# The second layer's normalisation tail, one round shorter: squares a round earlier, and inverse roots as one GpSimd power

## The chip, the cores and the metric

The kernel runs on one core of a Trainium2 chip. The core has five engines that run side by side, each through its own queue in order: TensorE (in the profile PE, with its weight loads as PEld), VectorE (DVE), ScalarE (ACT), GpSimd (POOL) and SyncE (SP), which here only issues DMAs. An instruction waits at the head of its queue until what it reads has been written and what it overwrites has been read; everything behind it waits too. The metric is the device time of one execution in microseconds, lower is better, given as the median over several runs.

## What is computed

Two transformer layers on an input `x` of 8 sequences with 256 rows of 512. Each is an attention and a feed-forward part, with residuals. The change lies in the attention of the second layer, an mLSTM with 16 heads of 32 columns; `q` is the normalised input, `k` and `v` are a given context:

```python
D = jnp.exp(log_D - max_log_D)
qk = jnp.einsum('bhsd,bhtd->bhst', qh, kh) / jnp.sqrt(dh)
C = qk * D
normalizer = jnp.maximum(jnp.abs(C.sum(-1, keepdims=True)), jnp.exp(-max_log_D))
Cn = C / (normalizer + EPS)
h = jnp.einsum('bhst,bhtd->bhsd', Cn, vh)
mu = h.mean(-1, keepdims=True)
var = ((h - mu) ** 2).mean(-1, keepdims=True)
hn = (h - mu) * jax.lax.rsqrt(var + EPS)
hn = hn * ln_scale.reshape(1, nh, 1, dh)
```

`x` plus this result is normalised again (a layer norm, then the RMS norm of the mixture of 32 experts that follows), routed to four experts a row, and added up.

## The kernel before, in words

The stages follow one another: first layer's attention (0 to about 235 us), its feed-forward part (to about 405 us), second layer's attention (to about 600 us), routing and the experts (to the end). Each stage begins while the former drains.

In the second layer's attention a **batch** is one sequence (256 rows, two tiles of 128 rows, j = 0 and 1, held in `g.X[2b]` and `g.X[2b+1]`), and a **block** is a batch and four of its heads. There are 32 blocks, and `round_` (L916) is called with a rising n. The order in which it issues work is kept as written on TensorE, ScalarE, VectorE and GpSimd (`manual_schedule`, L1040). A round n does, for different blocks at a time:

- `decays`: TensorE products and ScalarE exponentials for block n (`xe`, L732);
- `back` (L779): for block n - 3, the heads' results turned back to rows, and copied by ScalarE into `hid[b]` (L787);
- `weights` (L740): for block n - 1, TensorE's `pqk` (L747, L751), then on VectorE two products `ct` (L755);
- `heads` (L761): for block n - 2, TensorE's `num`, read from `ct`;
- `tail` (L867): the normalisation of the batches whose four blocks are done.

`hid[b]` is complete in round n = 6 + 4b. The tail of batch b counts r from there, so r = n - 6 - 4b, and in each round up to four batches are at different r, the older first (r of 8 and up, then 4 to 7, then 0 to 3; r of 12 and up at the round's end). Before the change:

- r = 0, `scales` (L794): ScalarE takes the absolute values of the normaliser's column, VectorE the maximum `nm` (L799).
- r = 1, `squares` (L802): GpSimd squares `hid` into `sq` (L805; for the last batch ScalarE, L807), ScalarE squares `nm` (L808).
- r = 2, `variance` (L811): VectorE sums `sq` by head (L812) and adds `nm` (L813).
- r = 3 and 4, `rsqrt` (L82): an inverse square root on VectorE from an integer guess and three Newton steps, 11 instructions of 128x36 (L89 to L94). 32 of the 36 columns are this batch's heads; the other four belong to the norms of the batch before it.
- r = 4: `shifts` (L830) makes those norms' offsets `nb` on VectorE (L832), with one small addition on GpSimd (L837). Then `attended` (L817): GpSimd multiplies `hid` by the roots (L819, 1,024 columns), and for each of the two tiles by `ln_scale` (L824) and adds it to `x` (L825).
- r = 6 and 7: VectorE's statistics of the two tiles (`norm_stats`, L101 and L102), and in r = 7 the two variances (L900, L901) into the four columns of the next batch's `var`. The last batch has no next one and takes its own `rsqrt` and `shifts` there (L902).
- r = 11 and 12, `normed` (L840): ScalarE writes the normalised tile `yn` (L843), GpSimd scales `x` (L844), SP stores `yn` to `h_d` (L847).
- r = 13 and 14, `turned` (L850): TensorE transposes the tile (`hT`, L854), ScalarE copies it (L856).

The blocks end with round 34; 15 rounds more drain the tail (L1042, `full` is 35). Into some of the drain's rounds `filler` (L1027) puts products of the shared expert on TensorE (`pgu` L961, `po` L981) with their VectorE parts (`act` L970, `x` L989). After the loop come the logits (L1003), the remaining fillers, routing and the experts.

GpSimd has two further pieces of work in this stage: in rounds 24 and 26 a product over 1,024 columns for the shared expert's weights (`scale_shared`, L1240). And from round 3 on each round takes one step of the second half of the gates (`Gates.chain`, L495; its steps on VectorE include L508 to L523, and the splits into three parts, L528 and L530).

Of the kernel before, what the change touches and what calls it, by code (L numbers as in the profile page):

```python
# [19 lines left out]
F32 = mybir.dt.float32  # L20
# [4 lines left out]
AF = mybir.ActivationFunctionType  # L25
ALU = mybir.AluOpType
# [4 lines left out]
P = 128  # L31
D = 512
KD = D // P
B = 8
# [47 lines left out]
def rsqrt(g, x, n):  # L82


    nc = g.nc
    r = g.small.tile([P, n], F32, tag="rsq", name="rsq")
    t = g.small.tile([P, n], F32, tag="rsqt", name="rsqt")
    ri = r.bitcast(I32)
    nc.vector.tensor_scalar(ri, x.bitcast(I32), 1, None, ALU.arith_shift_right)  # L89
    nc.vector.tensor_scalar(ri, ri, -1, 0x5F3759DF, ALU.mult, ALU.add)  # L90
    for n in range(3):
        nc.vector.tensor_mul(t, r, r)
        nc.vector.scalar_tensor_tensor(t, t, -0.5, x, ALU.mult, ALU.mult)
        nc.vector.scalar_tensor_tensor(r, t, 1.5, r, ALU.add, ALU.mult)  # L94
        yield r


def norm_stats(g, mv, x):

    st = g.small.tile([P, 6], F32, tag="st", name="st")  # L100
    g.nc.vector.bn_stats(st, x)  # L101
    g.nc.vector.bn_aggr(mv, st)  # L102
# [10 lines left out]
def setup(g, ctx, tc):  # L113
    nc = g.nc
    g.const = const = ctx.enter_context(tc.tile_pool(name="const", bufs=1, reuse_waits="tile"))
    g.small = ctx.enter_context(tc.tile_pool(name="small", bufs=4, reuse_waits="tile"))
    xp = ctx.enter_context(tc.tile_pool(name="resid", bufs=1, reuse_waits="tile"))
    g.X = [xp.tile([P, D], F32, tag=f"x{i}", name=f"x{i}") for i in range(NT)]

    g.ident = const.tile([P, P], F32, tag="ident", name="ident")  # L120
    make_identity(nc, g.ident)
    g.identb = const.tile([P, P], BF16, tag="identb", name="identb")
    nc.vector.tensor_copy(g.identb, g.ident)
    g.ones = const.tile([P, S], F32, tag="ones", name="ones")
    nc.vector.memset(g.ones, 1.0)
    g.eps = {}
    for n, v in (("ln", 1e-5), ("gn", 1e-3), ("n", 1e-6 * math.sqrt(1e-6)), ("magic", MAGIC), ("-magic", -MAGIC)):
        t = const.tile([P, 1], F32, tag=f"eps_{n}", name=f"eps_{n}")
        nc.vector.memset(t, v)
        g.eps[n] = t  # L130
# [545 lines left out]
def layer1_attention(g, tc, gates):  # L676
    nc = g.nc
    with ExitStack() as ctx:
# [19 lines left out]
        with tc.tile_pool(name="a1ps2", bufs=1, space=PSUM, reuse_waits="tile") as ps, tc.tile_pool(name="a1work", bufs=2, reuse_waits="tile") as work:  # L698
# [90 lines left out]
            shape = [P, 2 * H1, HD1]  # L789

            def flat(hid):
                return hid.rearrange("p j h d -> p (j h) d")[:, :, :HD1]

            def scales(b, hid):  # L794


                nm = g.small.tile([P, 2, H1], F32, tag="nm", name="nm")
                nc.scalar.activation(nm, hid[:, :, :, HD1], AF.Abs)
                nc.vector.tensor_max(nm, nm, em[:, :, b * H1 : (b + 1) * H1])  # L799
                return nm  # L800

            def squares(b, hid, nm):  # L802
                sq = work.tile(shape, F32, tag="sq", name="sq", bufs=1)
                if b + 1 < B:
                    nc.gpsimd.tensor_mul(sq, flat(hid), flat(hid))  # L805
                else:
                    nc.scalar.activation(sq, flat(hid), AF.Square)  # L807
                nc.scalar.activation(nm, nm, AF.Square, bias=g.eps["n"], scale=math.sqrt(1e-6))  # L808
                return sq

            def variance(var, sq, nm):  # L811
                nc.vector.tensor_reduce(var, sq, AX.X, ALU.add)  # L812
                nc.vector.scalar_tensor_tensor(  # L813
                    var, var, 1.0 / HD1, nm.rearrange("p j h -> p (j h)"), ALU.mult, ALU.add
                )

            def attended(b, hid, rs):  # L817

                nc.gpsimd.tensor_mul(flat(hid), flat(hid), rs.unsqueeze(2).to_broadcast(shape))  # L819
                for j in range(2):  # L820
                    i = 2 * b + j
                    hj = hid[:, j, :, :HD1]
                    x, scale = (t.rearrange("p (h d) -> p h d", d=HD1) for t in (g.X[i], lns))
                    nc.gpsimd.tensor_mul(hj, hj, scale)  # L824
                    nc.gpsimd.tensor_add(x, x, hj)  # L825
# [4 lines left out]
            def shifts(mv, rs):  # L830
                nb = g.small.tile([P, 2, 2], F32, tag="nb2", name="nb2")
                nc.vector.scalar_tensor_tensor(  # L832
                    nb, mv[:, :, 0].unsqueeze(1).to_broadcast([P, 2, 2]), -1.0,
                    rs.rearrange("p (n j) -> p n j", n=2), ALU.mult, ALU.mult,
                )

                nc.gpsimd.tensor_scalar(rs[:, :2], rs[:, :2], 1.0, None, ALU.add)  # L837
                return nb
# [11 lines left out]
            def turned(i, h):  # L850

                pt = ps.tile([P, CH], F32, tag="dec", name="hT", bufs=2).rearrange("p (k t) -> p k t", k=KD)
                for k in range(KD):
                    nc.tensor.transpose(pt[:, k, :], h[:, k * P : (k + 1) * P], g.ident)  # L854
                c, o = divmod(i * P, CH)
                nc.scalar.copy(qT[c][:, :, o : o + P], pt)  # L856
# [5 lines left out]
            V, hid, xe, ct, num, numT = {0: values(0)}, {}, {}, {}, {}, {}  # L862
            nm, sq, v, mv, nb, h, roots = {}, {}, {}, {}, {}, {}, {}
            end = KD - 1 + 3
            NV = 2 * H1

            def tail(n, r0, of):  # L867

                for r in (r0 + 4 * m for m in of):
                    b, rest = divmod(n - end - r, KD)  # L870
                    if rest or not 0 <= b < B:
                        continue
                    if r == 0:
                        nm[b] = scales(b, hid[b])
                    if r == 1:
                        sq[b] = squares(b, hid[b], nm[b])
                    if r == 2:
                        v[b] = g.small.tile([P, NV + 4], F32, tag="var", name="var")
                        variance(v[b][:, :NV], sq.pop(b), nm.pop(b))
                        if b == 0:  # L880
                            nc.vector.memset(v[b][:, NV:], 1.0)
                    if r == 3:
                        roots[b] = rsqrt(g, v[b], NV + 4)
                        next(roots[b])
                    if r == 4:
                        next(roots[b])
                        rs = v[b] = next(roots[b])
                        if b:
                            nb[b - 1] = shifts(mv[b - 1], rs[:, NV:])
                        attended(b, hid.pop(b), rs[:, :NV])  # L890
                    if r in (6, 7):
                        if r == 6:
                            mv[b] = g.small.tile([P, 2, 2], F32, tag="mv2", name="mv2")
                        norm_stats(g, mv[b][:, r - 6], g.X[2 * b + r - 6])
                        if r == 7:
                            if b + 1 == B:
                                v[B] = g.small.tile([P, NV + 4], F32, tag="var", name="var")
                                nc.vector.memset(v[B], 1.0)
                            rt = v[b + 1][:, NV:].rearrange("p (n j) -> p n j", n=2)
                            nc.vector.tensor_scalar(rt[:, 0], mv[b][:, :, 1], 1e-5, None, ALU.add)  # L900
                            nc.vector.tensor_scalar(rt[:, 1], mv[b][:, :, 1], 1.0 + 1e-6, 1e-11, ALU.mult, ALU.add)  # L901
                            if b + 1 == B:  # L902
                                *_, v[B] = rsqrt(g, v[B], NV + 4)
                                nb[b] = shifts(mv[b], v[B][:, NV:])
                    if r in (11, 12):
                        i = 2 * b + r - 11
                        h[i] = normed(i, v[b + 1][:, NV:].rearrange("p (n j) -> p n j", n=2), nb[b])
                    if r in (13, 14):
                        turned(2 * b + r - 13, h.pop(2 * b + r - 13))

            second = gates.chain(
                1, lambda: ps.tile([P, 2, CH], F32, tag="pqk", name="gates", bufs=2)[:, :, :S],
# [107 lines left out]
            for c in range(EARLY):  # L1020
                of = [(p, r) for p, r in chunk(c)]
# [17 lines left out]
            E_ = mybir.EngineType  # L1039
            with tc.manual_schedule(engines={E_.PE, E_.Activation, E_.DVE, E_.Pool}):  # L1040
                full = len(blocks) + 3
                for n in range(full + 15):  # L1042
                    round_(n)
                    if n >= full and n - full in (0, 1, 2, 4, 5, 8, 9):
                        filler()
                logits_turned(logits())
# [495 lines left out]
```

## Time and profile before

| | |
|---|---|
| median of 3 runs | 1127.02 us (1123.28, 1127.02, 1127.94) |
| the profiled execution's own time | 1118.39 us |
| its span, first to last instruction | 1116.6 us |
| granted TensorE clock over the span | 0.964 |
| TensorE busy | 1019.6 us (91%) |
| VectorE busy | 524.3 us (47%) |
| ScalarE busy | 396.4 us (36%) |
| GpSimd busy | 390.6 us (35%) |

The profile describes one execution. Its span leaves out 1.8 us that lie around the first and last instruction. It also gives, in slices or windows of time, how long each engine was busy and which share of the full TensorE clock was granted. The view of waits lists which instruction waited for which, with the sum, the number and the longest. The chain of waits follows the work that ended last back from the end of the program. In lines that describe groups, "x64" is the number of instructions, followed by busy time and mean duration, and by the idle time before them and what ended it. By stage, in windows (us):

| window | length | TensorE busy | VectorE busy | GpSimd busy | granted clock |
|---|---|---|---|---|---|
| 420.00 to 484.60 | 64.60 | 53.69 | 42.77 | 13.49 | 0.87 |
| 484.60 to 560.20 | 75.60 | 66.15 | 50.83 | 44.09 | 0.91 |
| 560.20 to 619.00 | 58.80 | 54.53 | 24.65 | 29.57 | 0.97 |
| 619.00 to 668.00 | 49.00 | 44.68 | 47.25 | 5.74 | 0.97 |
| 668.00 to 1116.60 | 448.60 | 430.19 | 90.97 | 216.52 | 0.98 |

The first two are the blocks of the second layer's attention, the third is the drain of its tail, the fourth the routing, the last the experts.

### The profile page before, as it was taken

What the parts mean: (1) busy time and instruction counts of PE and PEld (TensorE: products, weight loads), DVE (VectorE), ACT (ScalarE), POOL (GpSimd) and SP (SyncE); (2) the same over time, 40 slices, a digit from 0 to 9 for tenths busy, and PEclk for the clock granted to TensorE, in tenths of its full rate; (3) what the DMA queues carried; (4) which work ended last, traced back from release to release, by engine and by line L of the source; (5) the groups of instructions that cost most, each with busy time, mean ns of one, the idle gap of its engine ahead of it and who ended that gap; (6) DMA issues with size and microseconds to landing.
All of it is one profiled execution on the core that took longest, in us unless ns stands there. A gap on an engine that the chain in (4) does not pass through costs nothing.

```text
span 1116.6 us, 14778 instructions
## 1 busy us (share of the span) xinstructions
PE 1019.6 (91%) x5219; PEld 617.4 (55%) x5234; DVE 524.3 (47%) x1480; ACT 396.4 (36%) x680; POOL 390.6 (35%) x367
## 2 busy tenths in 40 slices
PE   7989799988999768798889899999999999999994
PEld 5756466643444344455544444555566666677782
DVE  6545545468988744876653893121211212121210
ACT  4455335145666455457542100221122222312111
POOL 0144522230000100346464203644555555545432
PEclk9999899999999988889899999999999999999997
DMA  9686411013222211212012234877777788899982
GB/s 348 252 282 223 140 65 48 1 29 71 54 53 54 46 48 42 66 61 69 30 47 104 62 138 137 196 183 194 199 203 198 193 212 215 237 233 241 233 217 35
DMA packets 101107, 152.31 MB, mean 136 GB/s; under 512 B 39684, under 2 KB 42372, under 8 KB 101000
## 3 DMA queue, kind: packets, MB, share of 16 engines
q1 hardware_dynamic: 81872, 106.68, 30.9%
q0 software_dynamic: 18912, 44.50, 18.2%
q8 instruction: 43, 0.70, 0.3%
q14 instruction: 40, 0.33, 0.1%
q10 hardware_dynamic: 240, 0.10, 0.0%
HBM read 110.42 MB, written 32.96 MB: 128 GB/s over the span
## 4 chain that ended last, share of the span: by engine, by line
PE 67%; DVE 11%; DMA 7%; POOL 5%; ACT 5%; issue 3%; SPq 0%; DVEq 0%; POOLq 0%; ACTq 0%
PE po L1291 13%; PE pg L1274 12%; PE pu L1274 12%; PE p L557 3%; PE pz L372 3%; PE pw L317 3%; PE pt L1331 3%; DMA hqT<-hq 2%; DVE ct L755 2%; DMA raw<-in_ctx 2%; PE pqk L747 1%; PE pd L727 1%; PE num L768 1%; PE po L981 1%; PE py L576 1%
## 5 line engine op out<-in xcount | busy, mean ns | idle before, releaser
L1279 DVE TENSOR_TENSOR act<-pu,sg 128x264 f32<-128x264 f32 (+22 forms) x68 | 31.9, 469 | 314.9 <-PE pu L1274 308.7
L1316 POOL DMA_INDIRECT xg<-h_d,tok_of x85 | 83.6, 983 | 198.5 <-DVE of L1326 63.8
L1335 POOL DMA_INDIRECT out_x<-eo,to x85 | 132.9, 1564 | 55.4 <-ACT eo L1373 34.9
L1291 PE MATMUL po<-w,act 128*128 128x512 f32 (+10 forms) x456 | 143.1, 490 | 0.0
L1274 PE MATMUL pg<-xT,w 128*128 128x216 f32 (+21 forms) x512 | 136.5, 410 | 0.8 <-issue 0.8
L1274 PE MATMUL pu<-xT,w 128*128 128x216 f32 (+21 forms) x512 | 133.3, 403 | 0.0
L1373 ACT ACTIVATE eo<-po,slotw 128x512 f32<-128x512 f32 (+10 forms) x114 | 65.7, 577 | 178.1 <-PE po L1291 171.7
L1274 PEld LDWEIGHTS pg<-xT,w 128*128 128x128 f32 x512 | 93.9, 191 | 34.2 <-issue 18.8
L1274 PEld LDWEIGHTS pu<-xT,w 128*128 128x128 f32 x512 | 96.8, 190 | 26.2 <-issue 5.6
L1278 ACT ACTIVATE sg<-pg 128x264 f32<-128x264 f32 (+22 forms) x68 | 28.5, 419 | 203.7 <-PE pg L1274 188.2
L1291 PEld LDWEIGHTS po<-w,act 128*128 128x128 f32 (+10 forms) x456 | 54.1, 155 | 57.4 <-issue 47.9
L557 PE MATMUL p<-wq,xqT 128*128 128x512 bf16 (+1 forms) x379 | 79.5, 361 | 3.2 <-DMA xqT<-xq 2.1
L755 DVE SCALAR_TENSOR_TENSOR ct<-pqk,xe 128x768 f32<-128x768 f32 x64 | 58.3, 952 | 38.1 <-PE pqk L751 19.5
L557 PEld LDWEIGHTS <-xqT 128*128 128x128 bf16 x384 | 36.7, 98 | 44.4 <-DMA xqT<-xq 6.4
L1332 DVE TENSOR_TENSOR xT<-pt,nw 128x512 f32<-128x512 f32 (+12 forms) x85 | 51.1, 601 | 21.5 <-PE pt L1331 21.5
L317 PE MATMUL pw<-wg,xnT 128*128 128x512 f32 x128 | 60.9, 621 | 0.0
L732 ACT ACTIVATE xe<-pd 128x512 f32<-128x512 f32 x96 | 54.6, 596 | 13.6 <-PE pd L728 12.7
L372 PE MATMUL pz<-wo,wyT 128*128 128x512 f32 x128 | 57.9, 595 | 1.6 <-ACT wyT L366 1.6
L1331 PEld LDWEIGHTS pt<-ident,xg 128*128 128x128 f32 (+15 forms) x340 | 39.2, 140 | 25.2 <-PE po L1291 10.5
L101 DVE BATCH_NORM_STATS2 st<-x 128x6 f32<-128x512 f32 x64 | 43.8, 685 | 16.1 <-POOL x L825 10.1
L1331 PE MATMUL pt<-ident,xg 128*128 128x128 f32 (+15 forms) x340 | 47.2, 260 | 1.7 <-DVE xT L1332 1.7
L576 PE MATMUL py<-wq,hqT 128*128 128x512 bf16 x168 | 41.2, 380 | 7.8 <-DMA hqT<-hq 7.4
(289 smaller groups left out, 1636.6 us busy)
## 6 DMA issues: line engine op xcount, KB each, us to landing
w<-in_w SPq DMA_DIRECT2D x32, 1024.0 KB
w<-in_w SPq DMA_DIRECT2D x32, 512.0 KB
wst<-in_w1T SPq DMA_DIRECT2D x8, 704.0 KB
wst<-in_w3T SPq DMA_DIRECT2D x8, 704.0 KB
wst<-in_w2T SPq DMA_DIRECT2D x6, 768.0 KB
x<-in_x SPq DMA_DIRECT2D x16, 256.0 KB
ctxT<-in_ctxT_d SPq DMA_DIRECT2D x4, 1024.0 KB
raw<-in_ctx SPq DMA_DIRECT2D x16, 256.0 KB
```

The source lines that it names most:

```text
L317: nc.tensor.matmul(pw, lhsT=xnT[c][:, k, o : o + P], rhs=wg[:, k, :], start=k == 0, stop=k == KD - 1)
L372: nc.tensor.matmul(pz, lhsT=wyT[:, k, :], rhs=wo[:, k, :], start=k == 0, stop=k == KD - 1)
L557: nc.tensor.matmul(pp[:, : z - a], lhsT=xqT[:, k, :], rhs=w[:, k, a:z], start=k == 0, stop=k == KD - 1)
L576: nc.tensor.matmul(py, lhsT=hqT[:, f, :], rhs=w2[:, f, :], start=f == 0, stop=f == NF - 1)
L732: nc.scalar.activation(out, pd, AF.Exp)
L755: nc.vector.scalar_tensor_tensor(ct[:, r : r + 2, :], pqk[:, :, : S + P], 1.0 / math.sqrt(HD1), xe[:, r : r + 2, :], ALU.mult, ALU.mult,)
L1274: nc.tensor.matmul(pp[:, :n], lhsT=w[:, k, cols], rhs=xT[:, k, :n], start=k == 0, stop=k == KD - 1)
L1291: nc.tensor.matmul(po[h * at : h * at + n, :cols], lhsT=act[:, m, j * P : j * P + n], rhs=w[:, m, h * cols : (h + 1) * cols], start=m == 0 ...
L1316: nc.gpsimd.indirect_dma_start(out=xg[:n], out_offset=None, in_=h_d, in_offset=bass.IndirectOffsetOnAxis(ap=g.tok_of[:n, r, j : j + 1], ax ...
L1331: nc.tensor.transpose(pt[:, k, :n], xg[:n, k * P : (k + 1) * P], g.ident[:n, :n])
L1335: return nc.gpsimd.indirect_dma_start(out=g.out, out_offset=bass.IndirectOffsetOnAxis(ap=rows, axis=0), in_=eo, in_offset=None, compute_op ...
L1373: nc.scalar.activation(eo[:n, at : at + cols], po, AF.Copy, scale=w[r][:n, j : j + 1])
```

## The change

Three things in `tail`, and one round less in the loop. The squares of a batch move from r = 1 to r = 0, the round in which its rows are complete; there they are issued before the former batch's second tile, since `attended` now takes a list of tiles, and only the first is issued with the scaling (r = 3), the second with the next batch's r = 0. The Newton steps for the 36 roots of a batch become one GpSimd instruction, a power with the exponent -0.5 from a constant tile; the last batch's own `rsqrt` stays. All later steps come a round earlier. ScalarE's square of `nm` moves into `variance`, and so stays in r = 1.

```diff
+def powers(g, x, n):
+    r = g.small.tile([P, n], F32, tag="rsq", name="rsq")
+    g.nc.gpsimd.tensor_tensor(r, x, g.neghalf[:, :n], ALU.pow)
+    return r
...
+    g.neghalf = const.tile([P, 40], F32, tag="neghalf", name="neghalf")
+    nc.vector.memset(g.neghalf, -0.5)
...
+                return sq
+
+            def variance(var, sq, nm):
                 nc.scalar.activation(nm, nm, AF.Square, bias=g.eps["n"], scale=math.sqrt(1e-6))
-                return sq
-
-            def variance(var, sq, nm):
                 nc.vector.tensor_reduce(var, sq, AX.X, ALU.add)
...
-            def attended(b, hid, rs):
-
+            def scaled(hid, rs):
                 nc.gpsimd.tensor_mul(flat(hid), flat(hid), rs.unsqueeze(2).to_broadcast(shape))
-                for j in range(2):
+
+            def attended(b, hid, of):
+                for j in of:
...
                     if r == 0:
                         nm[b] = scales(b, hid[b])
+                        sq[b] = squares(b, hid[b], nm[b])
+                        if b:
+                            attended(b - 1, hid.pop(b - 1), (1,))
                     if r == 1:
-                        sq[b] = squares(b, hid[b], nm[b])
-                    if r == 2:
                         v[b] = g.small.tile([P, NV + 4], F32, tag="var", name="var")
                         variance(v[b][:, :NV], sq.pop(b), nm.pop(b))
...
+                    if r == 2:
+                        roots[b] = powers(g, v[b], NV + 4)
                     if r == 3:
-                        roots[b] = rsqrt(g, v[b], NV + 4)
-                        next(roots[b])
-                    if r == 4:
-                        next(roots[b])
-                        rs = v[b] = next(roots[b])
+                        rs = v[b] = roots.pop(b)
                         if b:
                             nb[b - 1] = shifts(mv[b - 1], rs[:, NV:])
-                        attended(b, hid.pop(b), rs[:, :NV])
-                    if r in (6, 7):
+                        scaled(hid[b], rs[:, :NV])
+                        attended(b, hid[b], (0,) if b + 1 < B else (0, 1))
+                    if r in (5, 6):
...
-                    if r in (11, 12):
+                    if r in (10, 11):
...
-                    if r in (13, 14):
+                    if r in (12, 13):
...
-                for n in range(full + 15):
+                for n in range(full + 14):
```

## The prediction

> **What bounds the kernel now.** I read the chain of waits first: TensorE carries 67% of it, VectorE 11%, GpSimd 5%, and the GpSimd pieces lie only between about 480 and 590 us. That is the second layer's attention, 32 blocks in a hand-written order; nothing of the change lies outside it. Two adjacent stretches of windows frame it: from 484.6 to 560.2 us, 75.6 us hold 66.2 us of TensorE work at a granted clock of 0.91, although everything there is meant to keep TensorE busy. So what ends last inside a round?
>
> I count rounds by their pair of `ct` products (L755): round 8 starts at 445.90 us, round 16 at 484.65, round 24 at 521.73, round 32 at 560.18. Batch b's tail has r = n - 6 - 4b, so in every four rounds there is an R0 (n = 6, 10, ...), R1, R2, R3. What a round costs when only TensorE limits it is seen in the chain:
> ```profile
> 444.92 0.66 PE pqk L747 x8
> 448.30 0.66 PE pqk L747 x8
> ...
> 504.81 0.66 PE pqk L747 x8
> 509.11 0.66 PE pqk L747 x8
> ```
> 3.4 us plain, 4.3 us with the transposes of a tile of `hT`. Four rounds with two such tiles: 15.4 us. The sixteen rounds from 16 to 32 would be 61.6 us; they take 75.5. The timeline of GpSimd, then of VectorE, over one batch shows why (start, duration, engine, line; in brackets the idle time before and what ended it):
> ```profile
> 517.81 0.21 POOL L837 TENSOR_SCALAR rsq<-rsq 128x2 f32<-128x2 f32 x1 [6.49 <-DVE nb L832]
> 517.98 1.92 POOL L819 TENSOR_TENSOR hid<-hid,rsq 128x1024 f32<-128x1024 f32 x1
> 519.98 1.18 POOL L824 TENSOR_TENSOR hid<-hid,lns 128x512 f32<-128x512 f32 x1
> 521.23 1.19 POOL L825 TENSOR_TENSOR x<-x,hid 128x512 f32<-128x512 f32 x1
> 522.38 1.19 POOL L824 TENSOR_TENSOR hid<-hid,lns 128x512 f32<-128x512 f32 x1
> 523.65 1.19 POOL L825 TENSOR_TENSOR x<-x,hid 128x512 f32<-128x512 f32 x1
> 524.81 0.78 POOL L844 TENSOR_SCALAR x<-x,rsq,nb 128x512 f32<-128x512 f32 x1
> 525.54 1.90 POOL L805 TENSOR_TENSOR sq<-hid 128x1024 f32<-128x1024 f32 x1
> ```
> ```profile
> 521.73 1.82 DVE L755 SCALAR_TENSOR_TENSOR ct<-pqk,xe 128x768 f32<-128x768 f32 x2 [2.18 <-PE pqk L751]
> 523.47 0.68 DVE L101 BATCH_NORM_STATS2 st<-x 128x6 f32<-128x512 f32 x1
> 524.19 0.18 DVE L102 BATCH_NORM_AGGREGATE mv<-st 128x2 f32<-128x6 f32 x1
> 527.48 1.22 DVE L812 TENSOR_REDUCE var<-sq 128x32 f32<-128x1024 f32 x1 [3.11 <-POOL sq L805]
> 528.80 0.54 DVE L813 SCALAR_TENSOR_TENSOR var<-var,nm 128x32 f32<-128x32 f32 x1
> 529.27 1.81 DVE L755 SCALAR_TENSOR_TENSOR ct<-pqk,xe 128x768 f32<-128x768 f32 x2
> ```
> GpSimd was idle 6.49 us, then does its batch in one run, with the next batch's squares last. VectorE stands at `var` for 3.11 us, and the next `ct` is queued behind it, so TensorE starves: rounds 24 and 28 last 7.5 and 8.05 us. The waits and windows give the sum and the after-effect:
> ```profile
> DVE var L812 <- POOL sq L805: 11.1, 4, 4.0
> PEld pqk L747 <- DVE ct L755: 9.2, 5, 3.2
> ...
> 490.00:500.00 10.00, 7.31 (x44) 4.11 (x42) 8.20 (x23) 3.65 (x9) 1.99 (x4) 0.70 0.22 79
> 530.00:540.00 10.00, 9.38 (x87) 5.95 (x88) 7.96 (x23) 4.90 (x11) 3.33 (x5) 0.83 0.07 28
> ```
> After each gap the clock (third value from the right) sinks to 0.70 or 0.83, so a gap costs more than its own length.
>
> **Part one: the order on GpSimd.** Before, from `nb` (L832) to the end of the squares: 0.25 + 1.95 + 4 x 1.22 + 0.77 + 1.89 = 9.7 us (556.74 to 566.43 measures it). `var` stands two rounds after `nb`, at 6.7 to 7.6 us; the difference is the stall, 1.9 us more where a shared weight's product (L1240) comes between. After, the squares come behind the first tile: 0.25 + 1.95 + 2.45 + 1.89 = 6.55 us. `nb` moves to R3 and `var` to R1, again two rounds apart, and R3 + R0 last 3.4 + 4.3 us. `nb` ends at 2.0 us into R3; `var` comes after its round's `ct` and the first tile's statistics, 1.82 + 0.91 into R1: 8.4 us. The stall goes, with 1.9 us to spare. The second tile ends 9.0 us after `nb`; its statistics, in R2, come 12.7 us after. `normed` and `turned` each come a round earlier; their products on GpSimd (L844) wait for ScalarE work that follows the round's exponentials, and lie ahead of `nb`. On SP the two `h_d` stores now stand ahead of the next batch's loads, whose rows are wanted two rounds later: nothing.
>
> **Part two: the roots.** Gone from VectorE: 11 small instructions a batch, 0.225 us from start to start: 2.5 us, in rounds R3 and R0, which they lengthen to 3.94 and 3.87 us over TensorE's 3.4. That is about 0.5 us each. Added: one GpSimd power of 128x36. No power is in this trace, so it is bounded. Below: two-input products of 512 and 1,024 columns take 1.18 and 1.89 us, hence 0.47 us plus 1.39 ns a column, 0.52 us for 36. Above: eleven such passes, one for each Newton instruction, 5.7 us. Here the Trainium skill speaks against the change: "GPSIMD Engine Reference", section on engine selection, sends elementwise work to VectorE as about twice as fast, and its section on pitfalls prices a dependent float chain at 4 cycles an element and step. Taking some 25 steps as my estimate: 36 x 100 cycles at its 1.2 GHz, 3.0 us, plus 0.5. By the row, the power fits where GpSimd idles 5 to 8 us a batch; by the rule it is 3.5 us. I take **2 us**, nearer the row. When it matters: the power starts 3.0 us into R2 (`ct` 1.82, statistics 0.91, two small ones 0.25), and `nb` wants it 1.8 us into R3, 2.2 us later. VectorE has 1.4 us more before the next `ct` would be late, and GpSimd's path its 1.9. So up to 3.6 us it costs nothing; beyond, each microsecond comes back in some seven batches. The new wait is VectorE's, at `nb`; the next round's `ct` is queued behind it, and TensorE waits for that.
>
> **Part three: the start, rounds 8 to 16.** They take 38.75 us. Round 10 alone is 9.33: four VectorE instructions of the gates (L528, L530) take 1.15 to 2.02 us beside GpSimd's run, where without it they take 0.29 and 0.42. "SBUF — State Buffer", on its two separate sides, states the reason: a lock that VectorE takes for two SBUF inputs or its fast modes, held against GpSimd for a whole instruction. By the row for `ct` (one input from PSUM, 0.94 to 0.96 us throughout) the moved squares slow nothing else; if the lock held for `ct` too, four rounds of a batch would lose about a half pass of 0.6 us each, 2.4 us. The row decides. After, GpSimd has scaled batch 0 by then and only the second tile's two passes meet those casts: round 10 about 4.9 us, round 11 without its half clock 4 for 6.33, the earlier rounds even. That is 6 us (0 to 9).
>
> **Part four: the drain.** From round 32 to the logits 38.3 us pass, with TensorE idle 2.54 and 1.08 us for `act` (L970) and 1.8 us lost to the clock. By my count through the queues, the first `act` comes at 32's start + 16.4 us instead of 22.1, and TensorE wants it at 19.6: idle gone. The second now stands behind both tiles' statistics and the last Newton run (L902, kept): + 28.2, wanted at 25: idle 3.2. Net 1 us gained (-2 to +3), falling 2 us for each microsecond of the power, since two powers lie on that path. After it TensorE is full to 619 us, and routing and experts shift as a whole.
>
> **The sum.** Rounds 16 to 32: 75.5 - 61.6 = 13.9; I hold back 2, since R1 now has 4.2 us of VectorE work against TensorE's 4.3: 12 us. With 6 and 1: 19 us of the profiled 1118.4. That execution is 0.8% under the median of 1127.0, whose runs go from 1123.3 to 1127.9; the same share of 1.7% there gives **1108**.
>
> **Rivals.**
> - *The power is long* (slower). Change = -19 + 7 x (X - 3.6) + 2 x (X - 2): it turns at X = 5.4 us. At 8 us it is +24: 1151. For it: no row shows a power, and work lane by lane would be far above my bound. Against: GpSimd's other instructions on few columns take 0.2 to 0.6 us. 0.19.
> - *Another wait takes the place* (half the gain). GpSimd reaches the squares late again, R1 becomes VectorE's, or the gates' casts are hit twice: about 8 us gained, 1119. For it: R1's balance of 0.1 us. 0.18.
> - *The change doesn't bring what it says*: the squares come early but TensorE only waits later, in the drain or for routing, which starts at 620 us after the last shared product. Against: from 598 to 619 TensorE has no gap. Within 5 us, 1127: 0.08.
> - Forecast, 13 to 25 us gained: 0.55.
>
> About 0.5% (5.6 us) is what a measurement of this kernel tells from no change. Faster by more than that: 0.55 and most of the second, 0.69. Within: 0.11. Slower: 0.20. The range goes down to the full gain with a free power (27 us, 1100) and up past break-even to 1133, which leaves out the longest powers. The likeliest case alone: 1102 to 1114.
>
> **What would show it.** `var` without a GpSimd wait in rounds 16 to 32; those rounds in 61 to 64 us; their clock near 1.0; a GpSimd row of 128x36 under 3.6 us; round 10 near 5 us; `act` reached at once the first time and late the second. A `nb` that waits for GpSimd for several microseconds in every batch would make the prediction wrong, as would a power that slows VectorE beside it.

## The result, and the profile after

The changed kernel takes 1130.36 us (median of 15 runs, 1125.26 to 1136.47), the kernel before on the same chip 1122.57 us (15 runs, 1112.23 to 1127.94). The ratio is 1.0084, 95% interval [1.0059, 1.0110]: slower by about 9.4 us (by the medians alone 7.8). The predicted time was 1108.

The profiled execution of the changed kernel took 1127.19 us, its span is 1125.4 us (before 1116.6), its granted clock 0.963 (before 0.964). The chain of waits, by engine, then one row of the groups of instructions on its page:

```profile
PE 64%; POOL 10%; DVE 10%; DMA 9%; ACT 3%; issue 3%; SPq 0%; POOLq 0%; DVEq 0%; ACTq 0%
...
L100 POOL TENSOR_TENSOR rsq<-var,neghalf 128x36 f32<-128x36 f32 x8 | 49.4, 6178 | 25.9 <-DVE var L910 20.4
```

GpSimd's share of the chain doubled, from 5% to 10%, and 49.4 us of new work stand in one row: eight powers of 6.18 us each. The view of waits over the blocks, 485 to 562 us (who waited for whom: sum in us, number, longest):

```profile
DVE nb L841 <- POOL rsq L100: 17.9, 4, 4.5
...
DVE var L820 <- POOL sq L813: 3.8, 4, 0.9
```

VectorE's stall at `var` fell from 11.1 us to 3.8, as the change meant. In its place stands a stall of 17.9 us at `nb`, 4.5 us in every batch. How the two belong together is seen in the timelines of one batch. GpSimd:

```profile
507.07 6.15 POOL L100 TENSOR_TENSOR rsq<-var,neghalf 128x36 f32<-128x36 f32 x1 [2.20 <-DVE var L910]
...
513.96 0.22 POOL L846 TENSOR_SCALAR rsq<-rsq 128x2 f32<-128x2 f32 x1
514.14 1.91 POOL L826 TENSOR_TENSOR hid<-hid,rsq 128x1024 f32<-128x1024 f32 x1
...
518.53 1.90 POOL L813 TENSOR_TENSOR sq<-hid 128x1024 f32<-128x1024 f32 x1
...
525.79 6.15 POOL L100 TENSOR_TENSOR rsq<-var,neghalf 128x36 f32<-128x36 f32 x1 [2.20 <-DVE var L910]
```

VectorE in the same stretch:

```profile
513.25 0.16 DVE L841 SCALAR_TENSOR_TENSOR nb<-mv,rsq 128x4 f32<-128x4 f32 x1 [4.54 <-POOL rsq L100]
513.33 1.82 DVE L763 SCALAR_TENSOR_TENSOR ct<-pqk,xe 128x768 f32<-128x768 f32 x2
...
520.46 1.22 DVE L820 TENSOR_REDUCE var<-sq 128x32 f32<-128x1024 f32 x1 [0.94 <-POOL sq L813]
521.78 1.10 DVE L821 SCALAR_TENSOR_TENSOR var<-var,nm 128x32 f32<-128x32 f32 x1
522.81 1.81 DVE L763 SCALAR_TENSOR_TENSOR ct<-pqk,xe 128x768 f32<-128x768 f32 x2
...
525.54 0.16 DVE L910 TENSOR_SCALAR var<-mv 128x2 f32<-128x2 f32 x1
```

This is a **ring**: a chain of waits that comes back to where it began. Power (507.07), `nb` (513.25), scaling and first tile, squares (end 520.43), `var` (520.46), a pair of `ct`, statistics with L910 (end 525.70), next power (525.79). Each step waits for the one before it, or stands behind it in its engine's queue, and one turn takes 18.72 us: 13.4 on GpSimd, 5.4 on VectorE. A batch has four rounds, and by the prediction's estimate TensorE could do them in 15.4. In the turn GpSimd is busy for 16.3 us, so even with other waits it could not come down to 15.4. The clock of rounds 16 to 32 is 0.93, hardly over the 0.91 of before. The rounds again, counted by their pairs of `ct`, with the drain from round 32 to the end of its last shared product (the last run of L981 before, of L990 after), in us:

| stretch | before | after | after minus before |
|---|---|---|---|
| start to round 8 | 445.90 | 445.18 | -0.7 |
| rounds 8 to 16 | 38.8 | 40.2 | +1.4 |
| rounds 16 to 32 | 75.5 | 76.7 | +1.2 |
| drain, round 32 to the last shared product's end | 58.9 | 68.0 | +9.1 |
| from there to the end | 497.5 | 495.3 | -2.2 |

The sum is the 8.8 us between the spans. Most of it shows in the drain, where TensorE stands for the shared expert's `act` (timeline of TensorE, before, then after):

```profile
582.32 5.40 PE L961 MATMUL pgu<-qT,sw 128*128 128x512 f32 x8 [2.54 <-DVE act L970]
...
590.09 2.84 PE L981 MATMUL po<-sw,act 128*128 128x512 f32 x6 [1.08 <-DVE act L970]
```

```profile
587.29 5.40 PE L970 MATMUL pgu<-qT,sw 128*128 128x512 f32 x8 [2.99 <-DVE act L979]
...
598.77 2.08 PE L990 MATMUL po<-sw,act 128*128 128x512 f32 x2 [4.35 <-DVE act L979]
```

These are 7.3 us of idle time against 3.6 before. Both `act` stand on VectorE behind the tail, and the tail's last two powers, 6.14 us each, hold it up (`nb` waits 6.26 us for each of them). The idle time is only half of the loss. Over the whole drain TensorE is idle for 4.3 us before and 9.0 after, and busy for 54.6 us before and 59.1 after, while its granted clock goes from 0.97 to 0.87.

### The profile page after: what moved, and what is told of

Its sections match the earlier page's. It is cut to its first block, busy times and chain, and to the rows that moved or that the text cites. A ratio compares the mean times of both kernels' runs of the same rounds, so it can differ in the third digit from the quotient of the medians.

```text
span 1125.4 us, 14713 instructions
## 1 busy us (share of the span) xinstructions
PE 1024.3 (91%) x5234; PEld 620.4 (55%) x5234; DVE 518.6 (46%) x1393; ACT 398.0 (35%) x680; POOL 439.9 (39%) x375
## 4 chain that ended last, share of the span: by engine, by line
PE 64%; POOL 10%; DVE 10%; DMA 9%; ACT 3%; issue 3%; SPq 0%; POOLq 0%; DVEq 0%; ACTq 0%
PE po L1300 13%; PE pg L1283 12%; PE pu L1283 12%; POOL rsq L100 4%; PE p L565 3%; PE pz L380 3%; PE pw L325 3%; PE pt L1340 3%; DMA vc_d<-raw 3%; DMA hqT<-hq 2%; DMA raw<-in_ctx 2%; PE po L990 1%; POOL hid L826 1%; PE py L584 1%; DVE ct L763 1%
## 5 line engine op out<-in xcount | busy, mean ns | idle before, releaser
L380 PE MATMUL pz<-wo,wyT 128*128 128x512 f32 x128 | 57.9, 594 | 2.5 <-ACT wyT L374 2.5
L100 POOL TENSOR_TENSOR rsq<-var,neghalf 128x36 f32<-128x36 f32 x8 | 49.4, 6178 | 25.9 <-DVE var L910 20.4
```

The costliest lines, as they stand in the source:

```text
L100: g.nc.gpsimd.tensor_tensor(r, x, g.neghalf[:, :n], ALU.pow)
L380: nc.tensor.matmul(pz, lhsT=wyT[:, k, :], rhs=wo[:, k, :], start=k == 0, stop=k == KD - 1)
```

## The experiments

All ratios are to the kernel before on the same chip; "rounds 16 to 32" is from each kernel's profiled execution. In the diffs the lines with - are those of the kernel that the run starts from; `...` marks what is left out.

### The order alone: order_newton

The changed kernel with the Newton steps back on VectorE (first step in r = 2, the rest in r = 3).

```diff
                     if r == 2:
-                        roots[b] = powers(g, v[b], NV + 4)
+                        roots[b] = rsqrt(g, v[b], NV + 4)
+                        next(roots[b])
                     if r == 3:
-                        rs = v[b] = roots.pop(b)
+                        next(roots[b])
+                        rs = v[b] = next(roots[b])
```

> Only the new order; the roots stay Newton steps on VectorE (first step in r = 2, the rest in r = 3). Theory A, the length of the power (6.2 us) is what costs: without it the order gives what was predicted of it, 12 to 19 us off the kernel before, a ratio of 0.983 to 0.990, and var waits at most a few tenths for the squares. Rival B, the order itself costs (the second tile and its statistics come late, and the next power or Newton run with them): slower than before by 5 us or more. Rival C, it is GpSimd's work beside VectorE, slowed by each other, that costs: VectorE's small instructions stay at about 1 us instead of 0.2, and the gain is under 6 us.

Measured: 1111.87 us, ratio 0.9945 [0.9918, 0.9972]; rounds 16 to 32 take 65.7 us, rounds 8 to 16 40.3. Put beside the 1.0084 of the whole change, the power costs 1.4%, some 15.6 us, against the same order with Newton steps. The order is a gain, of 0.55% or about 6 us. That is less than the 12 to 19 us expected: with Newton steps L821 still takes 1.09 us a batch in these rounds, beside GpSimd's work, and round R1 lasts 5.05 us where TensorE needs 4.3. So the third view of the expectation holds in part.

### The roots alone: power_only

The kernel before with the power in place of the Newton steps, in the old order.

```diff
                     if r == 3:
-                        roots[b] = rsqrt(g, v[b], NV + 4)
-                        next(roots[b])
+                        roots[b] = powers(g, v[b], NV + 4)
                     if r == 4:
-                        next(roots[b])
-                        rs = v[b] = next(roots[b])
+                        rs = v[b] = roots.pop(b)
```

> Only the power, in the order before (issued in r = 3 where Newton began, used in r = 4). A: a batch becomes a ring of power 6.2, nb 0.2, GpSimd's run to the end of the squares 9.7, var 1.4, a pair of ct 1.8, statistics 1.2: 20.6 us against some 18.7 before, six times, and 3.7 us more twice in the drain and a few at the start: about 22 us slower than before (12 to 32), a ratio near 1.02. B: the power is not the cause, so 0 to 5 us slower, less than the changed kernel's 9.

Measured: 1139.59 us, ratio 1.0173 [1.0115, 1.0230]; rounds 16 to 32 take 83.2 us, round 32 to the last shared product's end 69.5. Both stalls are there now (waits of VectorE, 488 to 571 us):

```profile
DVE nb L840 <- POOL rsq L100: 18.2, 4, 4.5
DVE var L820 <- POOL sq L813: 15.8, 4, 5.4
```

The power adds its own stall and pushes GpSimd's run back, so that `var` waits longer than the 11.1 us of before. The two parts of the change pull in opposite directions: -0.55% and +1.73% alone, +0.84% together.

### The power's length: power_half, power_27, power_twice

power_half is the changed kernel with the power over 18 of the 36 columns and a copy of the other 18: it leaves those roots out. power_27 takes 27 and copies nine, whose roots it leaves out. power_twice issues the same power twice. The norms' four columns are the last of the 36, so in power_half and power_27 they lie in the copied part, and this turns out to matter.

```diff
-    g.nc.gpsimd.tensor_tensor(r, x, g.neghalf[:, :n], ALU.pow)
+    g.nc.gpsimd.tensor_tensor(r[:, : n // 2], x[:, : n // 2], g.neghalf[:, : n // 2], ALU.pow)
+    g.nc.gpsimd.tensor_copy(r[:, n // 2 :], x[:, n // 2 :])
```

```diff
                         roots[b] = powers(g, v[b], NV + 4)
+                        roots[b] = powers(g, v[b], NV + 4)
```

> The changed kernel with a power over 18 columns; the other 18 are copied, so these heads' roots and the norms' are left out. A, if the power's time goes with its columns: 3.1 to 3.4 us, at the edge of what was reckoned free: 12 to 18 us off the kernel before (0.984 to 0.990). A with a fixed cost: a power of still 5 us or more, and about the time before. B: as the changed kernel, 1.005 to 1.011.

> The changed kernel with a power over 27 columns; the other 9 are copied, so those roots are left out. From 3.27 us for 18 columns and 6.18 for 36 a column costs 0.161 us, so 4.7 us here. A, a free part up to 3.6 us and then each microsecond back in seven batches and twice more in the drain: -19 + 7 x 1.1 + 2 x 2.7 = 6 us under the kernel before (0 to 11), a ratio of 0.990 to 1.0. If instead the cost grew in step from the first microsecond, halfway between 18 and 36 columns: 3 to 4 us under it.

> The changed kernel with each batch's power issued twice in a row (the second is the one used). A: each of the batches in the blocks becomes 6.2 us longer, seven times, and the drain's two as well: some 50 us over the changed kernel (43 to 56), a ratio of 1.05 to the kernel before. B and C: GpSimd has idle time for it, so under 20 us.

| kernel | power a batch, us | rounds 8 to 16 | rounds 16 to 32 | ratio |
|---|---|---|---|---|
| power_half | 3.24 | 35.3 | 61.8 | 0.9849 [0.9799, 0.9900] |
| power_27 | 4.66 | 36.0 | 64.6 | not comparable |
| the changed kernel | 6.15 | 40.2 | 76.7 | 1.0084 [1.0059, 1.0110] |
| power_twice | 12.24 | 44.4 | 101.3 | 1.0507 [1.0455, 1.0559] |

power_27's total of 1668.87 us says nothing: with those roots left out its rows were routed so that the part for overfull experts ran (instructions that no other trace has), some 560 us. Its rounds come before the routing and can be read. (power_half leaves out norms' roots too, but it takes 495.3 us from the last shared product to the end, like the 495.3 of the changed kernel.)

From 6.15 to 12.24 us the four batches between rounds 16 and 32 lengthen by 24.6 us, that is 6.15 us a batch for 6.09 us of power: **each further microsecond of the power is a full microsecond of each batch**, as a ring demands.

The two short powers show less about the length, because they also open the ring. One batch of power_27, GpSimd's power and the last of VectorE's two small instructions that write the norms' variances:

```profile
495.08 4.67 POOL L101 TENSOR_TENSOR rsq<-var,neghalf 128x27 f32<-128x27 f32 x1
496.86 0.16 DVE L912 TENSOR_SCALAR var<-mv 128x2 f32<-128x2 f32 x1
```

The power begins 1.8 us before that instruction (L912 here, L910 in the changed kernel), where the changed kernel's power waits for it, 2.20 us, in the lines above; now only the copy behind the power reads the norms' columns. So at 3.24 us, with the ring open, the rounds take 61.8 us, the floor of 61.6 that TensorE is estimated to set, at a granted clock of 1.00, and the whole kernel is 1.5% faster than before. And power_27's 64.6 us are no longer a ring's: GpSimd is busy for 63.3 of them. From there to the changed kernel the rounds lengthen by 3.0 us a batch for 1.5 us of power. How much of that is the length, and how much the wait that comes back, is not shown: a short power that still waits for the norms' variances was not run.

A part of the turn lengthens besides, as the groups of VectorE show (mean ns of one before the last bar; before, then after, 485 to 562 us):

```profile
L813 DVE SCALAR_TENSOR_TENSOR var<-var,nm 128x32 f32<-128x32 f32 x4 | 1.1, 281 | 0.4
L799 DVE TENSOR_TENSOR nm<-nm,em 128x32 f32<-128x32 f32 x4 | 0.7, 184 | 0.0
```

```profile
L821 DVE SCALAR_TENSOR_TENSOR var<-var,nm 128x32 f32<-128x32 f32 x5 | 5.4, 1087 | 0.5
...
L807 DVE TENSOR_TENSOR nm<-nm,em 128x32 f32<-128x32 f32 x4 | 4.3, 1068 | 0.0
```

The same two instructions of 128x32 take 0.28 and 0.18 us before, 1.09 and 1.07 us after. Both read two inputs from SBUF, and in the order of the change they start when GpSimd is within a pass (for L807 the one from 514.14 to 516.05 us, for L821 the one from 521.64 to 522.83); each ends when that pass does, at 516.09 and 522.88. That is 1.7 us a batch, of which L821's 0.8 lies in the ring. In power_half the means of L821 and L807 are 0.53 and 0.71 us, in power_27 0.83 and 0.71. What this costs the changed kernel was not tried by itself; order_newton_nm below takes L821 away in the order with Newton steps.

The power itself does not stretch them. It stands on GpSimd from 444.05 to 450.46 us in the changed kernel, and VectorE's work on the gates within that time keeps its length; the same L807 that takes 1.07 us beside a product takes 0.18 within the powers of power_twice (449.08 to 461.61 us):

```profile
444.05 6.41 POOL L100 TENSOR_TENSOR rsq<-var,neghalf 128x36 f32<-128x36 f32 x1 [5.54 <-DVE var L891]
447.03 0.42 DVE L530 TENSOR_TENSOR sw<-sw 64x256 f32<-64x256 f32 x1
449.99 0.42 DVE L538 TENSOR_TENSOR sw<-sw,part 64x256 f32<-64x256 f32 x1
```

```profile
458.45 0.18 DVE L807 TENSOR_TENSOR nm<-nm,em 128x32 f32<-128x32 f32 x1
```

So a power that slows VectorE beside it, one of the prediction's signs of being wrong, is not what costs here.

### The drain alone: newton_last_two

The changed kernel, in which batches 6 and 7 have Newton steps and the first six a power.

```diff
                     if r == 2:
-                        roots[b] = powers(g, v[b], NV + 4)
+                        if b < 6:
+                            roots[b] = powers(g, v[b], NV + 4)
+                        else:
+                            roots[b] = rsqrt(g, v[b], NV + 4)
+                            next(roots[b])
...
```

> The changed kernel, but batches 6 and 7, whose roots lie in the drain, take Newton steps again. D, two powers one after the other in the drain are most of the loss, as the traces say (from round 32 to the last shared product 58.9 us before, 68.1 after): 7 to 9 us under the changed kernel, a ratio to the kernel before of 0.998 to 1.002. E, the loss lies in the blocks, and the drain is hidden by TensorE's other work: at most 3 us under the changed kernel.

Measured: 1121.37 us, ratio 1.0033 [1.0004, 1.0062]. Rounds 16 to 32 stay at 76.6 us, and from round 32 to the last shared product's end 57.2 us pass instead of 68.0. The two idle times of TensorE for `act` become one, of 0.57 us, and the clock of the drain is 0.92. By the ratios the drain's two powers cost 0.5%, 5.7 us, by the spans 8.3 us, so without them little of the changed kernel's loss is left, 0.33%.

### What a power costs: power_prices

The changed kernel with a row of powers of several widths, and one product, on an otherwise idle GpSimd at its start.

```diff
+        for n in (1, 4, 9, 18, 36, 72):
+            po = pp.tile([P, n], F32, tag=f"po{n}", name=f"po{n}")
+            nc.gpsimd.tensor_tensor(po, px[:, :n], pe[:, :n], ALU.pow)
...
+        nc.gpsimd.tensor_tensor(pm1, px[:, :36], pe[:, :36], ALU.mult)
...
+        nc.gpsimd.tensor_tensor(p11, g.ones[:, :36], pe[:, :36], ALU.pow)
```

> The changed kernel with eight more GpSimd instructions at the start, where GpSimd is idle: powers over 1, 4, 9, 18, 36 and 72 columns of 3.7, a product over 36, and a power over 36 columns of 1.0. Fixed 0.37 us and 0.161 us a column: 0.5, 1.0, 1.8, 3.3, 6.2 and 12.0 us; the product at 0.5 us as the line through the products of 512 and 1,024 columns gave; the power of ones at 6.2 us if its time doesn't depend on the values, well under it if it does.

The groups of GpSimd in the first 40 us (output, inputs, partitions x columns; the second number behind the bar is the mean in ns):

```profile
L141 POOL TENSOR_TENSOR po<-px,pe 128x72 f32<-128x72 f32 x1 | 11.9, 11867 | 0.0
L141 POOL TENSOR_TENSOR po<-px,pe 128x36 f32<-128x36 f32 x1 | 6.1, 6118 | 0.0
L145 POOL TENSOR_TENSOR p<-ones,pe 128x36 f32<-128x36 f32 x1 | 6.1, 6113 | 0.0
L141 POOL TENSOR_TENSOR po<-px,pe 128x18 f32<-128x18 f32 x1 | 3.2, 3209 | 0.0
...
L141 POOL TENSOR_TENSOR po<-px,pe 128x4 f32<-128x4 f32 x1 | 1.0, 1019 | 0.0
L141 POOL TENSOR_TENSOR po<-px,pe 128x1 f32<-128x1 f32 x1 | 0.6, 596 | 0.1
L143 POOL TENSOR_TENSOR pm<-px,pe 128x36 f32<-128x36 f32 x1 | 0.3, 253 | 0.0
```

One column takes 0.60 us and 72 take 11.87: (11.867 - 0.596) / 71 = 0.159 us a column, over some 0.44 us that do not depend on the width. A power of ones takes as long as one of 3.7. The product over the same 36 columns takes 0.25 us, a 24th of the power.

### The power outside the ring: power_off_ring

The changed kernel with the power in two pieces: the heads' 32 columns right behind `var` (r = 1), the norms' four in r = 3; the next batch's squares stand first in the round that ends its rows, then the scaling and both tiles. Later steps are a round later than in the changed kernel.

```diff
+                    if r == 4:
+                        if b + 1 < B:
+                            sq[b + 1] = squares(b + 1, hid[b + 1], None)
+                        rs = v[b] = roots.pop(b)
+                        if b:
+                            nb[b - 1] = shifts(mv[b - 1], rs[:, NV:])
+                        scaled(hid[b], rs[:, :NV])
+                        attended(b, hid.pop(b), (0, 1))
...
                     if r == 1:
...
+                        powers(g, v[b][:, :NV], roots[b][:, :NV])
...
-                    if r == 2:
-                        roots[b] = powers(g, v[b], NV + 4)
                     if r == 3:
+                        powers(g, v[b][:, NV:], roots[b][:, NV:])
```

> The power stays on GpSimd, but in two pieces: the heads' 32 columns (about 5.5 us) right after var in R1, and the norms' 4 columns (1.0 us) after the statistics in R3; in R0 the next batch's squares come first, then scaling and both tiles. So the chain var, power, nb, squares, var no longer closes a ring within four rounds. Theory (the ring of waits is what the power's length costs): VectorE's idle time at nb and var nearly goes, the sixteen rounds from 16 to 32 take 66 to 69 us instead of after's 76.7 (GpSimd's own work, about 17.0 us a batch, is then the limit: 4 x 17.0 = 68), and since the drain still has its two powers, the ratio to before is 0.994 to 1.003. Rival (GpSimd's occupied time, and VectorE slowed beside it, is what costs): these rounds stay at 74 to 77 us and the ratio at 1.005 to 1.010.

Measured: 1117.41 us, ratio 0.9978 [0.9948, 1.0009]; rounds 16 to 32 take 69.3 us, just above the 66 to 69 expected. The window over them (length, busy time of TensorE, its weight loads, VectorE, ScalarE, GpSimd, then clock and DMA share):

```profile
481.10:550.30 69.20, 59.56 (x706) 37.97 (x694) 49.90 (x73) 45.18 (x100) 67.87 (x44) 0.98 0.16 56
```

GpSimd is busy for 67.9 of 69.2 us. The two powers take no less time than before (5.44 and 1.00 us), and still 7.4 us of the 76.7 are gone: so they came from the order of the work, by the account above from the power's place in the ring, and not from its work as such. What stays over the floor of 61.6 is GpSimd's own work, which now fills the rounds. The run also puts the squares ahead of the scaling and the later steps a round later, and how much of the 7.4 us that brings was not tried apart.

### The squares alone: squares_first

The kernel before with its Newton steps; only the squares of the next batch come ahead of the scaling in R0, and `var` in R1.

```diff
                     if r == 0:
                         nm[b] = scales(b, hid[b])
+                        if b == 0:
+                            sq[b] = squares(b, hid[b], nm[b])
                     if r == 1:
-                        sq[b] = squares(b, hid[b], nm[b])
-                    if r == 2:
...
                             nb[b - 1] = shifts(mv[b - 1], rs[:, NV:])
+                        if b + 1 < B:
+                            sq[b + 1] = squares(b + 1, hid[b + 1], None)
                         attended(b, hid.pop(b), rs[:, :NV])
```

> The kernel before with one move alone: the next batch's squares are issued on GpSimd in R0 ahead of the scaling and both tiles, and var is in R1; the Newton steps stay on VectorE in R3 and R0, every later step stays in its old round. Theory (the squares' place behind the two tiles was the whole stall): no wait of var for GpSimd, rounds 16 to 32 take 63 to 67 us instead of 75.5, ratio 0.985 to 0.995, like order_newton (0.9945) or better, since R0 keeps its Newton steps off R2. Rival (the round that was gained for the later steps was needed too): ratio 0.997 or more, with the gain of these rounds given back by round 32's drain.

Measured: 1107.77 us, ratio 0.9894 [0.9864, 0.9924]; rounds 16 to 32 take 62.8 us. Waits of VectorE, 485 to 562 us:

```profile
DVE st L101 <- POOL x L825: 5.0, 6, 1.5
DVE ct L755 <- PE pqk L751: 3.0, 4, 1.2
DVE var L812 <- POOL sq L805: 1.8, 5, 0.4
```

`var` waits 0.4 us at most, and `ct` waits for TensorE, as it should where TensorE is the limit. From round 32 to the last shared product's end 57.9 us pass, so the old place of the later steps costs the drain nothing. This one move gains 1.1%, with the Newton steps kept. Its interval and order_newton's (0.9918 to 0.9972) overlap only at their ends, so the rest of the new order seems to take some of the gain back.

### One instruction less: order_newton_nm and squares_first_nm

The addition behind `var` (L821, 1.09 us in the changed order) goes: ScalarE writes the normaliser's square as a 33rd column of `sq`, so that the sum over 33 columns is the whole; the missing division by 32 is put into `ln_scale`.

```diff
-                nc.scalar.activation(nm, nm, AF.Square, bias=g.eps["n"], scale=math.sqrt(1e-6))
-                nc.vector.tensor_reduce(var, sq, AX.X, ALU.add)
-                nc.vector.scalar_tensor_tensor(
-                    var, var, 1.0 / HD1, nm.rearrange("p j h -> p (j h)"), ALU.mult, ALU.add
-                )
+                nc.scalar.activation(sq[:, :, HD1], nm.rearrange("p j h -> p (j h)"), AF.Square, bias=g.eps["n"], scale=math.sqrt(1e-6 * HD1))
+                nc.vector.tensor_reduce(var, sq, AX.X, ALU.add)
```

> The new order with Newton steps, and the normaliser's square written by ScalarE as a 33rd column of the squares, so that one reduction gives the variance, the addition after it (0.19 us alone, 1.09 us beside GpSimd) is gone, and a factor of the square root of 32 sits in ln_scale. If R1's VectorE work (5.0 us there against TensorE's 4.3) is what is left of the loss: rounds 16 to 32 in 62 to 64 us instead of 65.7, 2 to 5 us under the new order with Newton steps, a ratio to the kernel before of 0.989 to 0.994. If R2 and R3 with their Newton steps are the limit: no difference.

> squares_first and the one-instruction-less variance together: the normaliser's square goes as a 33rd column into sq (ScalarE writes it, ln_scale times the root of 32 makes up for the missing division), so VectorE's addition behind var is gone. If the addition still stands in a round that VectorE limits (R1 with ct, tile statistics and var), it takes up to 4 x 0.5 to 1 us from the sixteen rounds: 60 to 62 us instead of 62.8, ratio 0.985 to 0.989. If TensorE limits those rounds already (62.8 against a floor of 61.6), nothing is left to gain there: ratio as squares_first, 0.987 to 0.992.

Measured: order_newton_nm 1107.83 us, ratio 0.9896 [0.9846, 0.9946], rounds 16 to 32 63.2 us instead of order_newton's 65.7. squares_first_nm 1102.42 us, ratio 0.9872 [0.9823, 0.9920], rounds 16 to 32 63.0 us beside 62.8 without it: where TensorE already sets these rounds nothing is left to gain, and the intervals of squares_first and squares_first_nm do not tell the two apart. Against the kernel before they are 1.0% and 1.3% faster.

## Why the prediction was wrong

**The step that failed** is one term of the sum: "I take **2 us**, nearer the row". The power takes 6.18 us. Neither end held it: 0.52 us from the line through product rows, 5.7 us from eleven passes. The row was near in shape and engine, not in the operation: a product over these columns takes 0.25 us, a power 24 times that. The 4 cycles an element and step of the Trainium skill ("GPSIMD Engine Reference", "Performance pitfalls for Q7 kernels") gave an estimate of 3.5 us with my guess of 25 steps. That was the better warning, but 3.5 us lies within the 3.6 that the prediction counted as free, so it would have predicted a gain as well. At the page's 1.2 GHz the measured 0.159 us a column are some 190 cycles, by estimate, where I had put 100.

**The mechanism held; where it sets in is not shown.** The prediction named the wait at `nb`, with `ct` behind it, free up to 3.6 us, dear beyond. The wait is there in every batch, 4.5 us, and from 6.15 us on each microsecond of the power counts in full. The limit of 3.6 us was not tried, since both short powers also open the ring. If the turn of 18.72 us shrinks microsecond for microsecond, it comes down to 15.4 at a power of 2.8 us: an estimate, against the 3.6 of the prediction. With 6.2 us in place of 2, the rival's own formula gives -19 + 7 x 2.6 + 2 x 4.2 = +7.6 us; measured is +9.4. So "The power is long", held at 0.19, is what came, and its formula priced it well. Some luck is in how near: the formula's parts for rounds 16 to 32, -12 + 4 x 2.6 = -1.6 us, came out at +1.2, and routing and experts, put at nothing, gave 2.2 us back. Where between these lengths the change turns from gain to loss, which the formula puts at 5.4 us, no run shows.

**The order on GpSimd.** Predicted: the stall at `var` goes, 12 us gained in rounds 16 to 32 together with the roots off VectorE. With a power that hides, and the ring open (power_half), these rounds gain 13.7 us. With Newton steps (order_newton) they gain 9.8. What I had not priced is that L821 and L807 stretch beside GpSimd's passes; taking L821 away brings 2.5 us of the rest back (order_newton_nm, 63.2 us). The fear that R1 becomes VectorE's was right: R1 lasts 5.05 us in order_newton and 4.30 in order_newton_nm.

**The start.** Predicted: 6 us gained, round 10 about 4.9 us, round 11 about 4. In sum nothing of it came: round 10 fell from 9.33 us to 6.75, but round 9 went from 4.7 to 6.2, and the eight rounds take 40.2 us. The count that the casts escape GpSimd's run was wrong: four casts and splits are still held up, at 450.77, 452.83, 457.02 and 458.26 us (2.02, 1.16, 1.21 and 1.35 us), beside a run from 450.54 to 459.33. They are held in power_half and order_newton as well, so it is not the power's fault alone; the power of 444.05 to 450.46 us is in the way of the run, and with half of it power_half needs 35.3 us.

**The drain.** Predicted: 1 us gained, falling by 2 us for each microsecond of the power; with 6.15 us that is 8.3 - 1 = 7.3 us lost, measured 9.1. The count of the path was good: with 6.15 us the first `act` would come at round 32's start + 16.4 + 2 x 4.15 = 24.7 us and the second at + 36.5; TensorE goes on at + 25.2 and + 36.7. That the first would be reached at once was true only of a power of 2 us. newton_last_two, which takes both powers out, shows the predicted order, the first at once and the second late, by 0.57 us instead of 3.2; its drain is back at 57.2 us, 1.7 under before, near the 1 us predicted. What the count did not hold is TensorE's busy time in the drain, 4.5 us longer, at a granted clock of 0.87 instead of 0.97.

**The rest.** Routing and experts shift as a whole, as predicted: 2.2 us shorter after the last shared product (495.3 us; in the runs that can be compared 494.1 to 496.5, before 497.5).

## What to carry to other kernels

A new operation is priced by a row of that operation; a row of the same shape is no near row, and if none exists, say at which price the change turns and weigh the long side by that. Before an instruction moves to another engine, close the ring of waits that it stands in, and add up one full turn: once the turn is longer than the rounds it serves, every microsecond in it is paid in full; the same work outside the ring cost less here, and its limit was the engine's full time. A run that changes a length can also change a wait: look in its timeline for what each instruction still reads before you draw a line through it. And of a change in two parts, try each alone: here the order gained 0.55%, one part of it (the squares first) 1.1%, and the roots lost 1.7%.

## What was not expected of the hardware

- GpSimd's power in f32 over 128 partitions takes about 0.44 us and 0.159 us for each column, for both values tried (3.7 and 1.0); 36 columns last 6.12 us, the product 0.25 us.
- Beside GpSimd's two-input passes, VectorE's short instructions with two inputs in SBUF stretched to the end of the pass: 128x32 from 0.18 to 1.07 us and, in `var`'s addition, from 0.28 to 1.09. Even an instruction of 128x4 (`nb`) took 1.85 us once, at 531.97 us, against 0.16. The casts of the gates, with one input, stretched too (1.16 us against 0.29).
- Beside the power this was not seen: two-input instructions kept 0.42 and 0.18 us, the cast at 449.66 us its 0.29. `ct`, with one input in PSUM, keeps 1.82 us for its pair beside passes and power alike.
